# Layer 3 of a four-layer graph network: powers of the transition matrix replaced by Horner's rule

## The chip, the cores and the metric

The kernel runs on one core of a Trainium2 chip. The metric is the device time of one execution in microseconds (us). Of the kernel before there are three timed runs (median 2751.52 us, 2751.24 to 2751.78) and one profiled execution, whose trace is what everything here is read from. Differences below about 0.2% of this time can't be told from no change.

The engines are named as in the profile: PE is TensorE's matmul, PEld its weight load, DVE is VectorE, ACT is ScalarE, POOL is GpSimd, SP is the queue that issues nearly all transfers. Each engine works off its own instruction queue in order, and engines wait for each other by semaphores.

## The reference

A batch of 128 graphs of 64 nodes with 512 features passes through four layers. Each layer normalizes its input, applies a relu, and adds the result of a graph layer to `x`. Layers 0 to 2 are attention-like layers and are not touched. Layer 3 is a diffusion with two steps:

```python
e = jax.nn.leaky_relu(sj[:, None, :] + si[:, :, None] + ab[0], negative_slope=0.2)
alpha_matrix = A * jnp.exp(e)
transition = alpha_matrix / (jnp.sum(alpha_matrix, axis=-1, keepdims=True) + 1e-12)
Xk = X
for k in range(Wk.shape[0]):
    H = H + Xk @ Wk[k] + bk[k]
    Xk = jnp.einsum('bij,bjd->bid', transition, Xk)
return jax.nn.relu(H)
```

With P for the transition, H = X W0 + P X W1 + P P X W2 + biases. `sj` and `si` are two projections of X to one number for each node.

## The kernel before

All arithmetic is in float32. The 8192 tokens are worked in 32 blocks of 256 tokens: four graphs, two tiles of 128 partitions with two graphs of 64 nodes each. Layers 0 and 1 are done in pairs of blocks, then layer 2 for all blocks, then layer 3 for all blocks. The output of each layer goes to DRAM and is loaded again. Layer 3 of block 0 begins while layer 2 of its last two blocks (30 and 31) is still under way, since `layer3_in(0)` and `layer3_step(0)` are called from the loop over layer 2.

A product of a block's 256 x 512 activations with a 512 x 512 weight is done by Strassen's scheme in Winograd's form: seven quarter-size products, numbered 1 to 7, from four sums of the activations (`sums`, L215 to L218, on POOL) and four sums of the weight (formed once). The class `Product` issues them: two matmuls for each quarter product, accumulated in two PSUM banks, `ab` and `dc`. `keep_ab` and `keep_dc` (L275, L276, L283) copy half-done results aside, and `store` (L297 to L301) adds the pieces into the result. `side_by_side` runs two products at once and calls other work between their parts. There are four banks with the tag `mm`, so two products are open at a time. Further PSUM tiles have the tags `tr` and `sc`, two banks each.

Layer 3 of a block is spread over several functions. `layer3_norm` loads `x` and the adjacency, normalizes (L168 to L180), and takes the two projections (four instructions on L787, each a product of two SBUF tiles summed along the row). `layer3_in` spreads the projection over each graph with a matmul (L392, `sm_j`), makes the transition matrix, puts it into a block-diagonal 128 x 128 tile `bd`, gets its transpose and the transpose of its square by matmuls with `bd` (L833, `pn`), and multiplies both with the normalized activations (L849, `pz`, 16 matmuls of 64 rows), which gives PX and PPX, feature-major, in `z`. It then makes the four sums of Strassen's scheme for X, PX and PPX, twelve POOL instructions. `layer3_out` accumulates the three products X W0, PX W1 and PPX W2 in the same two banks, so that only one result is taken out (L276, L283, L878 to L890), then the relu and the sum with x (L895), then the store to `out` (L901). `layer3_step(b)` interleaves `layer3_out(b)` with `layer3_in(b + 1)` and `layer3_norm(b + 2)`. A scheduler places the instructions of each engine in its queue; where it moved something that matters, the text says so.

The tile `x` has four buffers. The load of block b + 4 (L58) can be issued only when the store of block b (L901) has landed.

Helpers that the change uses: `neighbour_sums` (L384) multiplies a tile of two graphs with the transposed adjacency weights in four matmuls of 64 x 64 x 512, each in another quadrant of TensorE; layers 0 and 1 use it (tiles `pa` and `po`). Layer 1 also takes its row sums with matmuls against a column of ones (L575, `den`), and `load_adjT` loads the transposed adjacency.

Of the kernel before, what the change touches and what calls it, by code (L numbers as in the profile page):

```python
# [8 lines left out]
FP = mybir.dt.float32  # L9
AF = mybir.ActivationFunctionType  # L10
# [15 lines left out]
def kernel(ctx: ExitStack, tc: tile.TileContext, a: dict, out: bass.AP):  # L26
# [22 lines left out]
    def tokens(ap):  # L49
        return ap.rearrange("(t p) d -> p t d", p=P)  # L50


    def rows(b: int):
        return slice(b * T, (b + 1) * T)
# [6 lines left out]
    def load_adjT(b: int, stage: int):  # L61
        adjT = med.tile([P, TT, N], FP, tag="adjT", name=f"adjT{stage}_{b}")
        nc.sync.dma_start(adjT, tokens(adjT_d[rows(b), :]))
        return adjT
# [36 lines left out]
    def weight(name: str, place: int, queue):  # L101
        w = fetched(name, place, queue)
        formed(w, nc.gpsimd)
        return w
# [40 lines left out]
        nc.vector.tensor_copy(eye[h, :], ident[h, h])  # L145
    neghalf = const.tile([P, TT], FP, tag="neghalf", name="neghalf")
    nc.gpsimd.memset(neghalf, -0.5)


    n_bd = 2  # L150
    bds = []
    for i in range(n_bd):
        e = const.tile([P, TT, P], FP, tag=f"bd{i}", name=f"bd{i}")
        nc.gpsimd.memset(e, 0.0)
        bds.append(e)
    turn = [0]

    def next_bd():
        turn[0] += 1
        return bds[turn[0] % n_bd]  # L160


    def norm(x, name: str):
# [225 lines left out]
    def graph_sums(e, cols: int, name: str):  # L389

        ps = ps_sc.tile([P, cols], FP, tag="sc", name=f"sm_{name}")
        nc.tensor.matmul(ps, ones_bd, e, start=True, stop=True)  # L392
        return ps
# [381 lines left out]
    def layer3_norm(b: int, source):  # L775


        x = load_x(b, source, 3)
        adj = med.tile([P, TT, N], FP, tag="adjT", name=f"adj3_{b}")
        nc.sync.dma_start(adj, tokens(adj_d[rows(b), :]))  # L780
        us, c3, _ = made3
        hs = norm(x, f"3_{b}")
        sij = small.tile([P, 2, TT], FP, tag="sij", name=f"sij_{b}")
        for s in range(2):
            for t in range(TT):
                hu = med.tile([P, D], FP, tag="agg", name=f"hu_{b}_{s}_{t}", bufs=2)
                nc.vector.scalar_tensor_tensor(  # L787
                    hu, hs[t], 1.0, us[s], ALU.mult, ALU.mult,
                    accum_out=sij[:, s, t : t + 1],
                )  # L790
        dj = small.tile([P, TT, N], FP, tag="e", name=f"dj_{b}")
        nc.vector.tensor_tensor(
            dj,
            eye.unsqueeze(1).to_broadcast([P, TT, N]),
            sij[:, 0, :].unsqueeze(2).to_broadcast([P, TT, N]),
            ALU.mult,
        )
        si = small.tile([P, TT], FP, tag="sj", name=f"si_{b}")
        nc.vector.tensor_scalar(si, sij[:, 1, :], c3, None, ALU.add)
        return x, adj, hs, dj, si  # L800

    def layer3_in(b: int, x, adj, hs, e, si, made: list):

        pj = graph_sums(e.rearrange("p t j -> p (t j)"), TT * N, f"j_{b}")
        hT = transposed(hs, f"3_{b}")
        nc.vector.tensor_tensor(
            e,
            pj.rearrange("p (t j) -> p t j", t=TT),  # L810
            si.unsqueeze(2).to_broadcast([P, TT, N]),
            ALU.add,
        )
        nc.vector.scalar_tensor_tensor(e, e, 0.2, e, ALU.mult, ALU.max)
        nc.scalar.activation(e, e, AF.Exp)
        nc.vector.tensor_tensor(e, e, adj, ALU.mult)
        den = small.tile([P, TT], FP, tag="den", name=f"den_{b}")
        nc.vector.tensor_reduce(den, e, AX.X, ALU.add)
        nc.vector.tensor_scalar(den, den, 1e-12, None, ALU.add)
        nc.vector.reciprocal(den, den)  # L820
        bd = next_bd()
        for g in range(2):
            h = slice(g * N, (g + 1) * N)
            nc.vector.tensor_tensor(
                bd[h, :, h], e[h], den[h].unsqueeze(2).to_broadcast([N, TT, N]), ALU.mult
            )
        yield
        tt = med.tile([P, TT, 2, N], FP, tag="tt", name=f"tt_{b}", bufs=2)
        for power in range(2):

            pn = ps_sc.tile([P, TT, N], FP, tag="sc", name=f"pn{power}_{b}")
            for t in range(TT):
                nc.tensor.matmul(  # L833
                    pn[:, t, :], bd[:, t, :], tt[:, t, 0, :] if power else eye,
                    start=True, stop=True,
                )
            nc.scalar.copy(tt[:, :, power, :], pn)
            yield
        z = big.tile([P, 2, K, T], FP, tag="qk", name=f"z_{b}")
        pz = [  # L840
            ps.tile([P, 2, K, N], FP, tag=tag, name=f"pz_{b}_{t}_{g}")
            for t, (ps, tag) in enumerate(((ps_tr, "tr"), (ps_sc, "sc")))
            for g in range(2)
        ]
        for t in range(TT):
            for c in range(K):
                for g in range(2):
                    h = slice(g * N, (g + 1) * N)
                    nc.tensor.matmul(  # L849
                        pz[t * 2 + g][:, :, c, :], hs[t][h, c * P : (c + 1) * P], tt[h, t],  # L850
                        start=True, stop=True,
                    )
        for i in range(2 * TT):
            nc.scalar.copy(z[:, :, :, i * N : (i + 1) * N], pz[i])

        other = ("e2", "pT", "pT" if b % 2 else "e2")
        made.append((x, [
            sums(m, f"3_{b}_{i}", ("S", other[i]))
            for i, m in enumerate((hT, z[:, 0], z[:, 1]))
        ]))  # L860
        yield

    def layer3_out(b: int, x, ops, stages):

        p = Product(f"y3_{b}")
        for i in range(3):
            p.early(ops[i], w3[i], (1, 6), i == 2)
        p.keep_ab()
        next(stages, None)
        for which in (5, 4):  # L870
            for i in range(3):
                p.early(ops[i], w3[i], (which,), i == 2)
            next(stages, None)
        p.keep_dc()

        bs = made3[2]
        y = big.tile([P, TT, D], FP, tag="v", name=f"y_{b}")
        nc.vector.tensor_tensor(y[:, 1, :F], p.d, bs[:, :F], ALU.add)  # L878
        nc.gpsimd.tensor_tensor(y[:, 0, F:], p.u2, bs[:, F:], ALU.add)
        nc.gpsimd.tensor_tensor(y[:, 1, F:], p.p5, bs[:, F:], ALU.add)  # L880
        for which in (2, 7, 3):
            for i in range(3):
                p.early(ops[i], w3[i], (which,), i == 2)
        nc.vector.tensor_tensor(p.u3, p.b, p.p1, ALU.add)
        y1 = y[:, 1, :].rearrange("p (j f) -> p j f", j=2)
        nc.vector.tensor_tensor(
            y1, y1, p.u3.unsqueeze(1).to_broadcast([P, 2, F]), ALU.add
        )
        nc.vector.tensor_tensor(y[:, 0, :F], p.a, bs[:, :F], ALU.add)
        nc.vector.tensor_tensor(y[:, 0, F:], p.c, y[:, 0, F:], ALU.add)  # L890

        to, last = tokens(out[rows(b), :]), b + 1 == n_blk
        whole = slice(0, D)
        for t, f in (1, whole), *([(0, slice(0, F)), (0, slice(F, D))] if last else [(0, whole)]):
            nc.vector.scalar_tensor_tensor(  # L895
                x[:, t, f], y[:, t, f], 0.0, x[:, t, f], ALU.max, ALU.add
            )
            if last:
                nc.sync.dma_start(to[:, t, f], x[:, t, f])
        if not last:  # L900
            nc.sync.dma_start(to, x)  # L901

# [61 lines left out]
            made2 = next(setup)  # L964


    w3, made_in = [], []
    made3 = normed3 = None

    def layer3_step(b: int, ahead: bool = True):  # L970


        nonlocal normed3
        stages = layer3_in(b + 1, *normed3, made_in) if b + 1 < n_blk else iter(())
        next(stages, None)
        if b + 2 < n_blk and ahead:
            normed3 = layer3_norm(b + 2, x2[b + 2])
        layer3_out(b, *made_in.pop(0), stages)

    qk, ops = layer2_in(0, normed2[0], [[], [end for _, end in open_end]])  # L980
    next(setup)
# [1 line left out]
    *_, v = values(0, ops)  # L983
    next(setup)
    turned2(1)
    w3 += [weight(f"L3_Wk{i}", 2 + i, nc.sync) for i in range(2)]
    for b in range(n_blk):
        x, adjq = loaded2[b]
        es = layer2_scores(b, adjq, qk)
# [6 lines left out]
        if b + 1 < n_blk:  # L996
            qk, ops = layer2_in(b + 1, normed2[b + 1])
        else:
            layer3_step(0, False)
        if b == n_blk - 2:  # L1000
            w3.append(weight("L3_Wk2", 4, nc.sync))
            next(stages)
        pTs = layer2_turned(b, es)
        if b + 1 < n_blk:
            prepare2(b + 2)
            coming = values(b + 1, ops)
            next(coming)
        next(stages, None)
        cT = layer2_context(b, v, pTs)
        part = out_part(b, x, cT)  # L1010
        if b + 1 < n_blk:
# [9 lines left out]


    for b in range(1, n_blk):
        layer3_step(b)


# [61 lines left out]
```

## Time and profile before

| what | value |
|---|---|
| timed runs, median (lowest to highest) | 2751.52 us (2751.24 to 2751.78) |
| profiled execution, its own time | 2750.76 us |
| profiled execution, span from first to last instruction | 2749.0 us |
| mean granted TensorE clock | 0.996 of full speed |
| weight loads, PEld, busy | 2352.7 us (86%) |
| layer 3 alone, 2060 to 2720 us: PE busy | 660.0 of 660 us |
| same stretch: DVE, ACT, POOL busy | 382.7, 167.8, 320.0 us |
| same stretch: DMA engines busy, mean | 14% |

The table's first rows differ a little: the profiled execution took 0.76 us less than the median of the timed runs, and its span leaves out 1.76 us around the instructions. A float32 matmul stands in the trace as two instructions; a group of `x24` is twelve matmuls. Durations of matmuls overlap in the trace, so the time that a group takes is read from the start of one group to the start of the next.

### The profile page before, as it was taken

How to read it: one execution, taken by the hardware profiler on the slowest of the kernel's cores; microseconds unless marked ns; L12 is line 12 of the kernel's file. 1: busy time of each engine (PE TensorE's matmuls, PEld its weight loads, DVE VectorE, ACT ScalarE, POOL GpSimd, SP SyncE). 2: the span in 40 equal slices, each digit the busy share in tenths (PEclk: the TensorE clock that was granted, in tenths of full speed). 3: DMA queues.
4: the chain of work that ended last, by engine and by line, in shares of the span. 5: the costliest groups of instructions: out<-in, count | busy, mean ns of one | idle time of the engine just before them, and what ended most of it. 6: DMA issues, size and time to landing. Idle time of an engine off the chain costs nothing.

```text
span 2749.0 us, 53245 instructions
## 1 busy us (share of the span) xinstructions
PE 2696.7 (98%) x21336; PEld 2352.7 (86%) x21336; DVE 1628.3 (59%) x4105; ACT 895.0 (33%) x2132; POOL 1279.6 (47%) x1648
## 2 busy tenths in 40 slices
PE   7899999999999999999999999999989999999999
PEld 5688888888888887899999999999878888888888
DVE  4466666666656667565655655556546555565553
ACT  2233333333333333333333333333322222222221
POOL 2433434343333436555555555554455444444443
PEclk9999999999999999999999999999999999999999
DMA  4111101001111113111111111111111111111110
GB/s 143 40 42 34 49 33 34 34 34 34 44 39 41 41 34 102 38 36 36 53 36 43 46 36 53 36 36 53 48 49 58 57 50 50 50 50 50 50 49 31
DMA packets 102488, 128.53 MB, mean 47 GB/s; under 512 B 40544, under 2 KB 50016, under 8 KB 102240
## 3 DMA queue, kind: packets, MB, share of 16 engines
q1 hardware_dynamic: 100576, 123.02, 13.3%
q8 instruction: 168, 2.75, 0.4%
q10 hardware_dynamic: 1664, 2.10, 0.2%
q14 instruction: 80, 0.66, 0.1%
HBM read 74.76 MB, written 50.33 MB: 46 GB/s over the span
## 4 chain that ended last, share of the span: by engine, by line
PE 87%; DVE 6%; POOL 3%; ACT 2%; DMA 1%; issue 1%; SPq 0%; DVEq 0%; ACTq 0%; POOLq 0%
PE ab_y L250 12%; PE ab_v L250 10%; PE dc_y L250 9%; PE dc_v L250 7%; PE ab_q L243 4%; PE ab_k L243 4%; PE tr L191 4%; PE ab_o L250 4%; PE ab_g L250 4%; PE dc_k L243 3%; PE dc_q L243 3%; PE dc_o L250 3%; PE ab_g L243 3%; PE dc_g L250 2%; PE pz L849 2%; PE dc_g L243 2%
## 5 line engine op out<-in xcount | busy, mean ns | idle before, releaser
L180 ACT ACTIVATE h<-x,nmr,rstd 128x512 f32<-128x512 f32 x256 | 196.5, 807 | 197.8 <-DVE nmr L175 197.6
L173 POOL TENSOR_TENSOR rstd<-ve,neghalf 128x2 f32<-128x2 f32 x128 | 89.4, 699 | 351.3 <-DVE ve L171 351.2
L250 PE MATMUL ab_v<-L_Wv,hT 128*128 128x256 f32 x768 | 200.6, 384 | 2.3 <-DVE u_v L276 1.3
L250 PE MATMUL ab_v<-L_Wv,S 128*128 128x256 f32 x768 | 198.5, 381 | 0.8 <-POOL S L216 0.8
L250 PE MATMUL dc_v<-L_Wv,S 128*128 128x256 f32 x768 | 197.6, 380 | 0.0
L250 PE MATMUL ab_y<-L_Wk,S 128*128 128x256 f32 x768 | 187.3, 380 | 0.0
L168 DVE BATCH_NORM_STATS2 stats<-x 128x6 f32<-128x512 f32 x256 | 165.4, 679 | 27.3 <-DMA x<-x 22.0
L250 PE MATMUL dc_y<-L_Wk,S 128*128 128x256 f32 x768 | 177.9, 381 | 0.0
L194 ACT COPY hT<-tr 128x512 f32<-128x512 f32 x128 | 74.7, 584 | 304.3 <-PE tr L191 280.2
L215 POOL TENSOR_TENSOR S<-hT 128x256 f32<-128x256 f32 x128 | 108.2, 845 | 130.5 <-ACT hT L194 125.0
L250 PEld LDWEIGHTS ab_v<-L_Wv,S 128*128 128x128 f32 x768 | 147.0, 192 | 21.8 <-POOL S L216 1.6
L250 PEld LDWEIGHTS ab_y<-L_Wk,S 128*128 128x128 f32 x768 | 146.5, 191 | 20.1
L250 PEld LDWEIGHTS dc_v<-L_Wv,S 128*128 128x128 f32 x768 | 146.4, 191 | 20.1
L250 PEld LDWEIGHTS dc_y<-L_Wk,S 128*128 128x128 f32 x768 | 143.6, 190 | 18.2
L191 PE MATMUL tr<-ident,h 128*128 128x128 f32 x1024 | 142.5, 280 | 15.5 <-ACT h L180 13.2
L196 DVE COPY hT<-tr 128x512 f32<-128x512 f32 x128 | 87.5, 684 | 110.6 <-PE ab_v L250 106.7
L250 PEld LDWEIGHTS ab_v<-L_Wv,hT 128*128 128x128 f32 x768 | 135.1, 193 | 16.5 <-DVE u_v L276 1.7
L678 POOL TENSOR_TENSOR e<-e,r 128x512 f32<-128x512 f32 x64 | 66.4, 1058 | 163.8 <-DVE r L677 163.8
L191 PEld LDWEIGHTS tr<-ident,h 128*128 128x128 f32 x1024 | 116.2, 142 | 28.9 <-ACT h L180 23.1
L250 PE MATMUL ab_y<-L_Wk,z 128*128 128x256 f32 x512 | 126.3, 379 | 0.0
L787 DVE SCALAR_TENSOR_TENSOR hu<-h,u 128x512 f32<-128x512 f32 x128 | 100.2, 817 | 27.2 <-ACT h L180 27.0
L301 POOL TENSOR_TENSOR gv<-u_g,p_g 128x256 f32<-128x256 f32 x32 | 23.3, 729 | 198.7 <-DVE u_g L298 198.7
(273 smaller groups left out, 6574.8 us busy)
## 6 DMA issues: line engine op xcount, KB each, us to landing
x<-x SPq DMA_DIRECT2D x128, 512.0 KB, 3.4
x<-in_x_dram SPq DMA_DIRECT2D x32, 512.0 KB, 3.6
out_dram<-x SPq DMA_DIRECT2D x31, 512.0 KB, 2.7
adjq<-in_adj_dram SPq DMA_DIRECT2D x64, 64.0 KB, 2.4
L_Wk<-in_L_Wk_dram SPq DMA_DIRECT2D x16, 256.0 KB, 4.2
adjT<-in_adjT_dram SPq DMA_DIRECT2D x32, 64.0 KB, 1.9
L_Wv<-in_L_Wv_dram SPq DMA_DIRECT2D x8, 256.0 KB, 5.3
adj<-in_adj_dram SPq DMA_DIRECT2D x32, 64.0 KB, 2.0
```

What stands on the lines that cost most here:

```text
L168: nc.vector.bn_stats(stats[:, t, :], x[:, t, :])
L173: nc.gpsimd.tensor_tensor(rstd, ve, neghalf, ALU.pow)
L180: nc.scalar.activation(h, x[:, t, :], AF.Relu, bias=nmr[:, t : t + 1], scale=rstd[:, t : t + 1])
L191: nc.tensor.transpose(pt[:, k, :], h[:, k * P : (k + 1) * P], ident)
L194: nc.scalar.copy(ht, pt)
L196: nc.vector.tensor_copy(ht, pt)
L215: nc.gpsimd.tensor_tensor(S1, A21, A22, ALU.add)
L243: nc.tensor.matmul(dst[:, m * P : (m + 1) * P], w[:, place, k, m * P : (m + 1) * P], left[:, k, :], start=key not in self.begun, stop=last ...
L250: nc.tensor.matmul(dst, left[:, k, :], w[:, place, k, :], start=key not in self.begun, stop=last and k == 1, skip_group_check=True,)
L678: nc.gpsimd.tensor_tensor(eh, eh, r.unsqueeze(2).to_broadcast([P, TT * hq, N]), ALU.mult)
L787: nc.vector.scalar_tensor_tensor(hu, hs[t], 1.0, us[s], ALU.mult, ALU.mult, accum_out=sij[:, s, t : t + 1],)
L849: nc.tensor.matmul(pz[t * 2 + g][:, :, c, :], hs[t][h, c * P : (c + 1) * P], tt[h, t], start=True, stop=True,)
```

## The change

Layer 3 is evaluated from the inside out: H = X W0 + P (X W1 + P (X W2)). All three products take X as their left operand, so only X is transposed and summed. The matrix product with P is done on token-major results, 128 x 512, by `neighbour_sums` in four quadrants, twice for each block (`po2` and `po3`). P isn't formed: the unnormalized weights `al`, transposed, are used, and the row sums, from four small matmuls `den`, divide afterwards (a per-partition scalar `r`). The tiles `bd`, `tt` and `z`, the matmuls `pn` and `pz`, their ACT copies, and eight of the twelve POOL sums go.

A step now has three parts. `layer3_head` runs the products X W2 and X W1 side by side, into `y12`. `layer3_tail` runs the product X W0, the row sums, and the first neighbour sum, which DVE scales by `r` and adds to X W1. `layer3_end` runs the second neighbour sum; ACT scales it, POOL adds X W0, DVE applies the relu and adds to x, and the store follows. The end of a block is called in the middle of the next block's head.

```diff
-        adj = med.tile([P, TT, N], FP, tag="adjT", name=f"adj3_{b}")
-        nc.sync.dma_start(adj, tokens(adj_d[rows(b), :]))
+        adjT = load_adjT(b, 3)
...
-        nc.vector.tensor_tensor(e, e, adj, ALU.mult)
-        den = small.tile([P, TT], FP, tag="den", name=f"den_{b}")
-        nc.vector.tensor_reduce(den, e, AX.X, ALU.add)
...
-            nc.vector.tensor_tensor(
-                bd[h, :, h], e[h], den[h].unsqueeze(2).to_broadcast([N, TT, N]), ALU.mult
-            )
+        al = small.tile([P, TT, N], FP, tag="am", name=f"al_{b}", bufs=2)
+        nc.vector.tensor_tensor(al, e, adjT, ALU.mult)
         yield
...
+        made.append((x, al, sums(transposed(hs, f"3_{b}"), f"3_{b}")))
+        yield
+
+    def layer3_head(b: int, ops, between):
+        y = big.tile([P, 2, TT, D], FP, tag="qk", name=f"y12_{b}")
+        side_by_side(*(
+            (ops, w3[i], None, lambda p, i=i: p.store(y[:, i - 1]), f"y{i}_{b}") for i in (2, 1)
+        ), between=between)
+        return y
+
+    def layer3_tail(b: int, al, ops, y):
+        p = Product(f"y0_{b}")
+        p.first(ops, w3[0])
+        p.second(ops, w3[0])
...
+        po = [ps_sc.tile([P, D], FP, tag="sc", name=f"po2_{b}_{t}") for t in range(TT)]
+        parts = neighbour_sums(po, al, [y[:, 1, t, :] for t in range(TT)])
+        r = small.tile([P, TT], FP, tag="r1", name=f"r3_{b}")
+        for t in range(TT):
+            nc.vector.tensor_scalar(r[:, t : t + 1], den[t], 1e-12, None, ALU.add)
+        nc.vector.reciprocal(r, r)
+        for t, to, at in parts:
+            nc.vector.scalar_tensor_tensor(
+                y[to, 0, t, :], po[t][at], r[at, t : t + 1], y[to, 0, t, :], ALU.mult, ALU.add
+            )
+        bs = made3[2]
+        y0 = big.tile([P, TT, D], FP, tag="v", name=f"y0_{b}")
+        nc.gpsimd.tensor_tensor(p.u2, p.u2, bs[:, F:], ALU.add)
+        nc.gpsimd.tensor_tensor(p.p5, p.p5, bs[:, F:], ALU.add)
         yield
+        p.late(ops, w3[0])
+        nc.vector.tensor_tensor(y0[:, 0, :F], p.a, bs[:, :F], ALU.add)
+        nc.vector.tensor_tensor(p.u3, p.b, p.p1, ALU.add)
+        nc.vector.tensor_tensor(y0[:, 1, :F], p.d, p.u3, ALU.add)
+        nc.gpsimd.tensor_tensor(y0[:, 1, F:], p.u3, p.p5, ALU.add)
+        nc.vector.tensor_tensor(y0[:, 0, F:], p.c, p.u2, ALU.add)
+        nc.gpsimd.tensor_tensor(y0[:, 1, :F], y0[:, 1, :F], bs[:, :F], ALU.add)
+        yield r, y0
+
+    def layer3_end(b: int, x, al, y, r, y0):
+        po = [ps_sc.tile([P, D], FP, tag="sc", name=f"po3_{b}_{t}") for t in range(TT)]
+        tz = [med.tile([P, D], FP, tag="pT", name=f"tz_{b}_{t}", bufs=3) for t in range(TT)]
         to, last = tokens(out[rows(b), :]), b + 1 == n_blk
+        for t, out_at, at in neighbour_sums(po, al, [y[:, 0, t, :] for t in range(TT)]):
+            nc.scalar.activation(tz[t][out_at], po[t][at], AF.Copy, scale=r[at, t : t + 1])
+        for t in range(TT):
+            nc.gpsimd.tensor_tensor(tz[t], tz[t], y0[:, t, :], ALU.add)
             nc.vector.scalar_tensor_tensor(
+                x[:, t, :], tz[t], 0.0, x[:, t, :], ALU.max, ALU.add
             )
...
+        y = layer3_head(b, ops, [[begin], [ending.pop()], [lambda: next(stages, None)]])
+        yield
+        tail = layer3_tail(b, al, ops, y)
+        next(tail)
+        yield
+        r_y0 = next(tail)
+        ending.append(lambda: layer3_end(b, x, al, y, *r_y0))
```

As built, the queues of steps 3 to 28 repeat. TensorE's queue for one step b is: products 1 and 6 of X W2, the spread of the projection (`sm_i`), products 5 and 4 of X W2, then 1, 6, 5, 4 of X W1, the second neighbour sum of block b - 1 (`po3`), the late part (2, 7, 3) of X W2, eight transposes for block b + 1, the late part of X W1, products 1, 6, 5, 4 of X W0, `den`, the first neighbour sum `po2`, and the late part of X W0. On DVE, the statistics for block b + 3 stand after `keep_ab` of X W0 and before the row sums' reciprocal; the four projections stand between the instructions that take out X W0 and the next step's. On SP, the load of x for block b + 4 still follows the store of block b.

## Prediction, made before the changed kernel ran

> **What bounds the kernel now.** I read the page first, then TensorE's order of time in layer 3, then the same view for layer 1, which already has the operation that the change brings in.
>
> ```profile
> PE 2696.7 (98%) x21336; PEld 2352.7 (86%) x21336; DVE 1628.3 (59%) x4105; ACT 895.0 (33%) x2132; POOL 1279.6 (47%) x1648
> ```
>
> TensorE is busy 98% of the span, and it makes 87% of the chain that ended last. One step of layer 3 on it, from the order of time (start us, us):
>
> ```profile
> 2197.25 1.03 PE L250 MATMUL ab_y<-L_Wk,S 128*128 128x256 f32 x4
> 2198.12 0.55 PE L833 MATMUL pn<-eye,bd 128*128 128x64 f32 x4
> 2198.51 2.81 PE L250 MATMUL dc_y<-L_Wk,S 128*128 128x256 f32 x12
> ...
> 2204.28 2.06 PE L849 MATMUL pz<-tt,h 64*128 64x128 f32 x32
> 2206.27 1.13 PE L250 MATMUL ab_y<-L_Wk,hT 128*128 128x256 f32 x4
> ...
> 2214.36 1.04 PE L191 MATMUL tr<-ident,h 128*128 128x128 f32 x8
> 2215.24 1.03 PE L250 MATMUL ab_y<-L_Wk,hT 128*128 128x256 f32 x4
> ```
>
> No gap: the step repeats every 22.30 us (2192.93 to 2215.24). From start to start, a quarter-product matmul takes 0.432 us (0.865 for the `x4`, two matmuls), the 42 of them 18.13; `sm_j` 0.22; transposes 0.88; `pn` 2 x 0.39; `pz` 1.99; sum 22.00. The other 0.30 are slow edges: about 0.1 before and after `pz`, which uses 64 rows of the array, and about 0.05 around each `pn`.
>
> **Steady steps on TensorE.** The 42 matmuls, `sm` and the transposes stay: 19.23 us. `pn`, `pz` and their edges go: 3.07 us. What comes is in layer 1's trace:
>
> ```profile
> 824.88 1.03 PE L250 MATMUL dc_v<-L_Wv,hT 128*128 128x256 f32 x4
> 825.83 0.29 PE L575 MATMUL den<-ones_bd,e 64*64 64x1 f32 x8
> 825.97 1.07 PE L384 MATMUL po<-v,e 64*64 64x512 f32 x8
> 826.97 1.13 PE L250 MATMUL ab_g<-fold,hT 128*128 128x256 f32 x4
> 827.94 1.03 PE L250 MATMUL ab_g<-fold,S 128*128 128x256 f32 x4
> ```
>
> `den` 0.14, `po` 1.00, and 0.09 and 0.10 of edge (0.95 and 0.97 where 0.865 is usual). So `po3` costs 1.20, `den` with `po2` 1.34, sum 2.54. A step needs 19.23 + 2.54 = 21.77 us, 0.53 less. A rule speaks against more switches: the Trainium skill, "TensorEngine Tiling (Array Packing)", Key Properties, says that changing the tiling mode drains TensorE. It gives no price there; "TensorE: Matmul & The Clock Gate", Single matmul latency, has a constant of some 166 ns for a matmul's issue and drain. An estimate with that at four edges instead of my 0.1 gives 22.0 us a step. The rows are of the same operation in the same surroundings, so I take 0.1.
>
> From the first matmul of step 1 to the last of step 31, before takes 2745.4 - 2059.12 = 686.3 us. After: 31 x (18.13 + 2.54) + 29 x 1.10 (two steps have no `sm` and transposes) = 672.7. **Gain 13.6 us.**
>
> **Can the other engines hold 21.77?** POOL loses eight sums of 0.72 and gains four 256-column adds of 0.73 and two 128x512 adds: no bound. ACT loses four 128x512 and two small copies (2.6 us) and gains as much. DVE I laid out in its queue order with the rows' durations: some 17 us in a step, no bound either, but it is in a ring. The store of block b must land before x of block b + 4 loads; its statistics stand in DVE's queue before the row sums; behind them come the four projections, then `exp` on ACT, then the scaling of `po3` on ACT, POOL's add, DVE's relu and the next store. Before, this ring has slack (DVE idles 4.9 us on `ab_y`). Its transfer leg is seen here:
>
> ```profile
> 2192.59 0.68 DVE L895 SCALAR_TENSOR_TENSOR x<-y,x 128x512 f32<-128x512 f32 x1
> ...
> 2199.46 1.29 DVE L168 BATCH_NORM_STATS2 stats<-x 128x6 f32<-128x512 f32 x2 [0.26 <-DMA x<-x]
> ```
>
> From 2193.27 to 2199.46: 6.2 us (SP's queue keeps store, then load; the adjacency behind them is needed two steps later). DVE from the statistics to the leaky relu: statistics 1.2, aggregate, `ve` and reciprocal 0.65, two small reads of `den` 0.45, three `po2` adds (as L584, 0.75, spaced 0.68) and `nmr` 2.2, wait for `rstd` 0.1, four projections at 0.70 2.8, five 256-column ops at 0.34 1.7, two small ones 0.5: 9.6. Then `exp` 0.35; three copies of 256 columns that stand before the scaling in ACT's queue 1.0; three scaled copies, priced between the plain copy (0.585) and the activation with two operands (0.807), at 0.6: 1.9; POOL's second add 1.1 (L678's 1.04; L991's 1.27 is the other end); relu 0.7; and 0.6, since POOL's second add waits for the relu of the first tile. Sum 21.5, which is 0.3 under 21.77.
>
> The last 0.6 is lock behaviour that the trace shows: a DVE op with two SBUF inputs (L886, alone 0.68) takes 1.30 beside POOL's adds. The add of bias on POOL (`d`-quarter, two adds back to back) falls on the third projection in the same way; if POOL goes first the ring is 22.1. So a step is 21.8 to 22.1; I take 21.9, costing 29 x 0.13 = **3.8 us**. Behind the waiting statistics DVE has the adds of `po2` and the taking-out of X W0; the next step's X W1 needs those banks. The tightest is `ab`, read some 3.0 us into the next step and needed at 3.7, so the wait is covered; with 0.7 more it would be TensorE's.
>
> **Layer 2 to 3.** Here before loses time:
>
> ```profile
> 2013.27 0.76 PE L191 MATMUL tr<-ident,h 128*128 128x128 f32 x5
> 2017.93 0.49 PE L392 MATMUL sm_j<-dj,ones_bd 128*128 128x128 f32 x2 [3.90 <-DVE e L661]
> ...
> 2018.80 1.91 PE L250 MATMUL ab_y<-L_Wk,hT 128*128 128x256 f32 x4
> 2020.51 1.65 PE L250 MATMUL ab_y<-L_Wk,S 128*128 128x256 f32 x4
> ...
> 2047.81 0.66 PE L691 MATMUL tr<-ident,e 128*128 128x128 f32 x4 [3.09 <-POOL e L678]
> ```
>
> `sm_j` waits for a bank that the softmax of layer 2's last block reads; that waits for POOL's updates of x, queued behind eight sums of `z`. Those sums go, so the softmax starts with the scores; and `sm_i` stands behind 1.7 us of matmuls. I take the 3.9 as gone, with the slow 1.45 us behind it. The second softmax half no longer stands behind layer 3's `ab` in DVE's queue, so the 3.09 goes too. Walking the new queues with these durations: the scores end near 2010.0, not 2013.27 (`pz` and the two `pn` out; the transposes only move); step 0 runs unbroken, 20.7 us, to 2030.7, against 29.5 us to 2042.75; layer 2's tail takes 11.8 (about 2 us idle on copies and `S_c`) against 16.4. Step 1 starts near 2042.5, not 2059.12: **gain 16.6 us.**
>
> New is a wait in step 1. x of block 3 takes the buffer of layer 2's last block, stored only at about 2045.3, so its statistics come 6.2 us later at 2051.5. DVE's queue there has statistics, two relus and four projections ahead of taking out X W2: that ends near 2059.6, while X W0 wants the banks at 2055.6. TensorE waits 4.0, the transposes and the tail behind it. Would its clock fall too? After the 3.90 wait above eight instructions took 3.2 us where 1.73 is usual, 1.45 lost. The skill's page on the clock gate (Part 1) says that one idle window of some 3.4 us halves the rate for as long, up to 1.7, or nothing where the wait straddles windows. I take 1.4: **loss 5.4 us** (0 to 8).
>
> **The ends.** Before ends 3.6 us after its last matmul (2745.4 to 2749.0). After: `po3` 1.2, ACT 2.0, POOL's second add 1.1, relu 0.7, transfer 2.7: 7.7. **Loss 4.1.** At the start `nmr` of block 0 no longer stands behind a wait for `mcol` on DVE: gain 0.3 at most; I take it.
>
> **Sum.** -13.6 + 3.8 - 16.6 + 5.4 + 4.1 - 0.3 = -17.2 us. From the profiled execution's 2750.76 that is 2733.6 (its span of 2749.0 falls to 2731.8); from the median, 0.76 higher, 2734.3. I predict 2734.
>
> **The rivals.**
> *TensorE alone paces*, the lock falls well and step 1 hardly waits: 2734 - 3.8 - 4 = 2726. For it: the ledger's 0.3 of slack. Against: back-to-back POOL ops beat the waiting DVE op in the trace. With the forecast's own middle this is one family, 2724 to 2742: 0.75.
> *The transition gives nothing* (its waits move to other releasers): 2734 + 16.6 - 5.4 = 2745. Against: the releasers named are removed. 0.08.
> *The ring paces at some 22.5*, all scaled copies at 0.8 and POOL's adds at 1.27: 29 x 0.6 more, 2751, no change. 0.11.
> *Slower: the lock.* If POOL's adds blocked three projections of each step, 3 x 0.55 on the ring's 21.5, the step is 23.1 and the time 2734 + 29 x 1.2 = 2769. It is even with before at 22.5 a step and slower beyond 22.7. Against: two of the adds wait for results that DVE makes between those projections. 0.05.
> *The work does not shrink*: the quadrants don't overlap here. Layer 1 shows eight in 1.00 us, so 0.01; 2760.
>
> A measurement tells 0.2%, 5.5 us, from no change: faster 0.85, same 0.09, slower 0.06. The range, 2720 to 2748, takes in the first two cases and half the third, with step 1's wait from none to 8.
>
> **What would show it.** Right: TensorE without gaps in steady steps, 21.8 to 22.1 us from `po3` to `po3`; `po` 1.0 us; statistics of x waiting about 2 us for DMA in each step; no wait at step 0, one of 3 to 5 us at step 1 before X W0; some 7.7 us after the last late matmul. Wrong: a regular TensorE wait on DVE, or a step at 22.3 or more.

## The result, and the profile after

| | kernel before | changed kernel |
|---|---|---|
| timed runs, median (lowest to highest), six each | 2751.38 us (2749.5 to 2751.84) | 2735.84 us (2733.86 to 2737.46) |
| ratio, 95% interval | | 0.9943 (0.993 to 0.9956) |
| profiled execution, span | 2749.0 us | 2734.2 us |
| mean granted TensorE clock | 0.996 | 0.994 |

The change gains 15.5 us, 0.57%. The prediction was 2734.0 with a range of 2720 to 2748. The two spans differ by 14.8 us, where the prediction's sum was 17.2.

The page's first row answers to the one of before: busy time, share of the span and instructions of each engine.

```profile
PE 2678.9 (98%) x20824; PEld 2275.4 (83%) x20824; DVE 1689.9 (62%) x4360; ACT 941.9 (34%) x2228; POOL 1279.7 (47%) x1582
```

TensorE has 17.8 us less to do, VectorE 61.6 and ScalarE 46.9 us more; POOL is where it was. TensorE is still busy 98% of a shorter span. A steady step in TensorE's order of time (start us, us; the start of the next row tells how long a group took):

```profile
2279.95 1.04 PE L178 MATMUL tr<-ident,h 128*128 128x128 f32 x8
...
2286.01 1.03 PE L237 MATMUL dc_y<-L_Wk,hT 128*128 128x256 f32 x4
2286.96 0.29 PE L823 MATMUL den<-ones_bd,al 64*64 64x1 f32 x8
2287.10 1.07 PE L371 MATMUL po<-y,al 64*64 64x512 f32 x8
2288.10 1.13 PE L237 MATMUL ab_y<-L_Wk,hT 128*128 128x256 f32 x4
2289.07 1.03 PE L237 MATMUL ab_y<-L_Wk,S 128*128 128x256 f32 x4
...
2301.73 1.04 PE L178 MATMUL tr<-ident,h 128*128 128x128 f32 x8
```

From transposes to transposes it is 21.78 us, with no wait. The granted clock is 1.00 from 2100 to 2720 us in both kernels, so steady steps are compared at one clock. `po` takes 1.00 us, `den` 0.14, the edges 0.09 (0.95 from 2286.01) and 0.10 (0.97 from 2288.10), as in layer 1. Of the 28 distances between successive `sm_i` from step 2 on, 26 are 21.77 or 21.78; the other two are 22.04 and 21.85.

The same step on the other engines, in order of time, shows the ring of the prediction:

```profile
2288.21 1.29 DVE L155 BATCH_NORM_STATS2 stats<-x 128x6 f32<-128x512 f32 x2 [2.04 <-DMA x<-x]
...
2295.07 1.23 DVE L773 SCALAR_TENSOR_TENSOR hu<-h,u 128x512 f32<-128x512 f32 x1
...
2297.36 0.28 DVE L798 SCALAR_TENSOR_TENSOR di<-di 128x128 f32<-128x128 f32 x1
...
2299.14 2.09 ACT L857 ACTIVATE tz<-po,r 128x512 f32<-128x512 f32 x3 [0.28 <-PE po L371]
...
2301.37 1.65 POOL L859 TENSOR_TENSOR tz<-tz,y 128x512 f32<-128x512 f32 x1 [0.20 <-ACT tz L857]
...
2303.06 0.69 DVE L860 SCALAR_TENSOR_TENSOR x<-tz,x 128x512 f32<-128x512 f32 x1 [1.16 <-POOL tz L859]
```

Read it as a loop: relu's end to the next statistics 6.24 us (2303.75 to 2288.21 + 21.78), statistics to the end of the leaky relu 9.43, on to the scaled copies 1.50, to relu's end 4.61; together 21.78. In that loop the one wait for something that is not in it is ScalarE's, 0.28 us for `po` from TensorE. So the ring itself needs 21.50, TensorE sets the pace, and the ring is right behind it.

Step 1, the one place in layer 3 where TensorE stands for over 1 us:

```profile
2058.06 0.29 PE L823 MATMUL den<-ones_bd,al 64*64 64x1 f32 x8
2063.03 2.08 PE L237 MATMUL ab_y<-L_Wk,hT 128*128 128x256 f32 x4 [4.69 <-DVE u_y L285]
2064.90 1.91 PE L237 MATMUL ab_y<-L_Wk,S 128*128 128x256 f32 x4
2066.61 1.55 PE L237 MATMUL dc_y<-L_Wk,S 128*128 128x256 f32 x4
2068.00 1.03 PE L237 MATMUL dc_y<-L_Wk,hT 128*128 128x256 f32 x4
```

A wait of 4.69 us, and behind it three groups that take 1.87, 1.71 and 1.39 us where 0.865 is usual: 2.4 us more. The clock had fallen while TensorE still waited. The profile by stretches shows it (from:to, length, busy us of PE, PEld, DVE, ACT and POOL with the number of instructions, then the granted clock, the DMA share and GB/s):

```profile
2060.84:2063.03 2.19, 0.00 (x0) 0.00 (x0) 2.19 (x10) 0.04 (x1) 0.00 (x0) 0.50 0.43 166
2063.03:2067.67 4.64, 4.64 (x11) 3.75 (x12) 2.31 (x10) 0.37 (x1) 1.41 (x2) 0.50 0.33 113
```

Before and behind these 6.83 us the clock is 1.00. Half of the 4.64 us in which matmuls ran is the time lost. The 3.9 and 3.1 us waits of before are gone, and step 1 starts at 2044.66 instead of 2059.12.

### The profile page after: what moved, and what is told of

It reads as the page before. It is cut to its first block, busy times and chain, and to the rows that moved or that the text cites. A ratio compares the mean times of both kernels' runs of the same rounds, so it can differ in the third digit from the quotient of the medians.

```text
span 2734.2 us, 52778 instructions
## 1 busy us (share of the span) xinstructions
PE 2678.9 (98%) x20824; PEld 2275.4 (83%) x20824; DVE 1689.9 (62%) x4360; ACT 941.9 (34%) x2228; POOL 1279.7 (47%) x1582
## 4 chain that ended last, share of the span: by engine, by line
PE 85%; DVE 5%; POOL 4%; DMA 2%; ACT 2%; issue 1%; SPq 0%; POOLq 0%; ACTq 0%; DVEq 0%
PE ab_y L237 12%; PE ab_v L237 10%; PE dc_y L237 9%; PE dc_v L237 7%; PE ab_q L230 4%; PE ab_g L237 4%; PE ab_k L230 4%; PE ab_o L237 4%; PE tr L178 4%; PE po L371 3%; PE dc_k L230 3%; PE ab_g L230 3%; PE dc_q L230 3%; PE dc_o L237 3%; PE dc_g L237 3%; PE dc_g L230 2%
## 5 line engine op out<-in xcount | busy, mean ns | idle before, releaser
L237 PE MATMUL ab_y<-L_Wk,hT 128*128 128x256 f32 x768 | 205.1, 390 | 5.3 <-DVE u_y L285 4.7
L237 PEld LDWEIGHTS ab_y<-L_Wk,hT 128*128 128x128 f32 x768 | 138.5, 190 | 72.3 <-issue 25.2
L237 PE MATMUL ab_y<-L_Wk,S 128*128 128x256 f32 x768 | 198.0, 380 | 0.0
L237 PE MATMUL dc_y<-L_Wk,S 128*128 128x256 f32 x768 | 197.7, 380 | 0.0
L859 POOL TENSOR_TENSOR tz<-tz,y 128x512 f32<-128x512 f32 x64 | 91.8, 1435 | 142.7 <-ACT tz L857 140.7
L237 PEld LDWEIGHTS ab_v<-L_Wv,hT 128*128 128x128 f32 x768 | 135.1, 193 | 16.6 <-DVE u_v L263 1.8
```

The source lines that it names most:

```text
L237: nc.tensor.matmul(dst, left[:, k, :], w[:, place, k, :], start=key not in self.begun, stop=last and k == 1, skip_group_check=True,)
L859: nc.gpsimd.tensor_tensor(tz[t], tz[t], y0[:, t, :], ALU.add)
```

## Experiments

Each kernel ran beside the kernel before on its own chip; so ratios are compared, and times only roughly. Layer 3 begins up to 5 us earlier or later from one kernel's execution to another's (the same instruction, the first `sm_i`, starts at 1979.59 in the longer ring below and at 1984.34 in the kernel with held statistics). A difference of a few us between two spans is therefore looked for in the stage where the edit is.

**A fifth buffer for x.** Is step 1's wait the buffer that layer 2's last block holds?

```diff
-        x = big.tile([P, TT, D], FP, tag="x", name=f"x{stage}_{b}", bufs=4)
+        x = big.tile([P, TT, D], FP, tag="x", name=f"x{stage}_{b}", bufs=5)
```

> The changed kernel with five buffers for x instead of four. Theory: the 4.7 us wait in step 1 of layer 3 is x of block 3, which needs the buffer that layer 2's last block stores; with a fifth buffer it takes that of the block before, and the wait and the 2.4 us of slow clock behind it go. Step 1 falls from 28.0 to about 21 us, the steady step stays at 21.8 (TensorE paces it), and the time falls by some 7 us from 2735.8 to about 2729. Rival: the wait comes from the length of DVE's queue (statistics, relus, projections ahead of taking out X W2), then over 3 us of it stay and the time is 2733 or more.

Measured 2730.29 us (2729.33 to 2733.07), ratio 0.9929 (0.9917 to 0.9942). TensorE in step 1:

```profile
2060.76 1.19 PE L237 MATMUL ab_y<-L_Wk,hT 128*128 128x256 f32 x4 [2.04 <-DVE u_y L285]
2061.74 1.91 PE L237 MATMUL ab_y<-L_Wk,S 128*128 128x256 f32 x4
2063.45 1.86 PE L237 MATMUL dc_y<-L_Wk,S 128*128 128x256 f32 x4
2065.14 1.03 PE L237 MATMUL dc_y<-L_Wk,hT 128*128 128x256 f32 x4
```

The wait falls from 4.69 to 2.04, but not to nothing, and the slow clock stays: two groups at 1.71 and 1.69, at a granted clock of 0.50 (2061.70 to 2065.11). The rest is on VectorE:

```profile
2054.99 1.29 DVE L155 BATCH_NORM_STATS2 stats<-x 128x6 f32<-128x512 f32 x2 [3.48 <-DMA x<-x]
```

The scheduler used the fifth buffer to put each load and its statistics one block further ahead. So it is now the statistics of block 4 that stand in VectorE's queue at this point, and x of block 4 takes the buffer that layer 2's last block holds. In steady steps nothing changes either: statistics wait 33.3 us for their loads in the last 15 such steps (32.5 in the changed kernel), 21.78 us a step. The wait has two parts, a buffer and an in-order queue, and a buffer alone moves the queue along with it.

**The statistics of block 4 held back in step 1.** Does the other part go if VectorE's queue there holds nothing that waits?

```diff
+        if behind is not None:
+            nc.vector.tensor_copy(stats[:, :, 0], behind)
...
-                normed3 = layer3_norm(b + 2, x2[b + 2])
+                normed3 = layer3_norm(b + 2, x2[b + 2], kept.get(b - 1))
...
+        if b == 1:
+            kept[b] = y[:, 0, 1, 0:TT]
```

> The changed kernel with a fifth buffer for x (2730.3 us alone) and the statistics of block 4 held behind step 1's two higher products (two columns of the product copied into the statistics' tile, which the statistics then overwrite), so that VectorE's queue in step 1 holds nothing that waits for a load; the queues of TensorE and SyncE are those of the kernel with the fifth buffer. Theory (what is left of step 1's wait is those statistics at the head of VectorE's queue, 3.48 us for their load): the 2.04 us wait falls under 0.5 us and the some 1.7 us of slow clock behind it go; step 2 may pay under 1 us for statistics that now come in a heap: 2726 to 2728 us. Rival (the wait has another cause, or the heap stops step 2 for as long): 2730 us or more.

Measured 2730.73 us (2728.96 to 2734.52), ratio 0.9926 (0.9914 to 0.9939): no different from the fifth buffer alone. Step 1 is clean: no wait and no slow clock, 30.40 us between the two `sm_i` around it, where the fifth buffer alone has 34.38 and the changed kernel 37.72. But the next four distances are 24.40, 22.49, 21.88 and 22.27 us. Around step 2 TensorE waits twice, 1.09 us each, the second time for a bank that the first neighbour sum's add reads:

```profile
2093.75 0.49 PE L381 MATMUL sm_i<-di,ones_bd 128*128 128x128 f32 x2 [1.09 <-DVE y L836]
```

The held statistics and projections of blocks 4 and 5 come in a heap, and the statistics behind them wait 4.28 us for their load. So the theory is right about the place, the rival about the sum: of the 4.0 us won in step 1, 2.6 + 0.7 + 0.1 + 0.5 are given back in the next four.

**The scores of layer 2's last block without the POOL sums (on the kernel before).** Is it the eight sums of `z` that held the softmax? For block 0 the products take quarters of `z` in place of their four sums each, so this block's result is another one.

```diff
+            if b == 0:
+                o = dict(ops[0])
+                zz = z[:, i - 1]
+                o[1], o[2] = (zz[:, 0:2, :P], B11), (zz[:, 2:4, :P], B21)
+                o[4] = (zz[:, 2:4, P:], T4)
+                ops.append(o)
```

> The kernel before with the eight POOL sums of z left out for block 0 alone (the products of block 0 with W1 and W2 then take X's sums in their place, so their values are not the reference's; the matmuls stay in number and shape). Theory: TensorE's wait of 3.9 us at the beginning of step 0, with 1.45 us of slow clock behind it, comes from POOL's backlog of these sums ahead of layer 2's updates of x; they go, and step 0 begins some 5 us earlier: 2746. The later 3.1 us wait on the second half of the softmax may stay, since DVE's queue order causes it. Rival: DVE's queue alone delays the softmax of the last block; then the 3.9 us stay and the time is within 1 us of 2751.4.

Measured 2744.63 us (2742.01 to 2748.59), ratio 0.998 (0.9973 to 0.9987): 5.4 us faster than before on the same chip. Both waits are gone (3.90 and 3.09), and POOL begins its update of x at 2011.80, right behind the sums of X. A new wait is in step 0:

```profile
2028.04 1.09 PE L833 MATMUL pn<-eye,bd 128*128 128x64 f32 x4 [2.84 <-DVE bd L824]
```

So the sums did hold the softmax, as the prediction said. Taking them out gives 5.4 us net. The new wait and the 6.63 us behind it at a granted clock of 0.50 (2028.04 to 2034.67) take back some 6.2 of what was won (an estimate from the two: 2.84 and half of 6.63). The changed kernel has no `bd` to wait for. The other 11 us of the transition's gain weren't taken apart by a run; in the trace `pz`, `pn` and this wait are what else is gone there.

**The quadrants taken back.** Each neighbour sum is two 128x128 matmuls on a block-diagonal tile, so the quadrants' overlap is gone. TensorE's other work stays; besides, ScalarE and VectorE take each sum out in two pieces instead of three, and `al` is written in two halves.

```diff
-        for t in range(TT):
-            for g in range(2):
-                nc.tensor.matmul(
-                    ps[t][half[g ^ t]], e[half[g], t, :], us[t][half[g]], start=True, stop=True
-                )
+        for t in range(TT):
+            nc.tensor.matmul(ps[t], bd[:, t, :], us[t], start=True, stop=True)
```

> The changed kernel with one thing put back: each neighbour sum is two 128x128 matmuls of 512 columns on a block-diagonal tile (its other blocks zeroed once), not four quadrants; the denominators likewise two matmuls on a column of ones. Same outputs computed, Horner's rule kept. Theory (steady step paced by TensorE, and the quadrants' overlap is real work saved): a sum costs 1.73 us (two of the earlier kernel's 0.87 us matmuls) in place of 1.0 plus 0.2 of edges, two sums a step, so a step grows from 21.78 to about 22.8 us and the kernel from 2734 to about 2766 us. Rival (the quadrants save nothing that sets the pace, because something other than TensorE paces): steps stay near 21.8 us, 2734 us; the copies of half a tile also go, so that it could even gain a little.

Measured 2775.94 us (2774.93 to 2777.29), ratio 1.0094 (1.0077 to 1.0111). This version doesn't compute what its expectation says: with two block-diagonal tiles in turn, a block's weights are overwritten before its second sum has read them. So it ran again with three:

> The neighbour sums as block-diagonal matmuls again, now with three block-diagonal tiles in turn instead of two (with two, a block's weights were overwritten by those of two blocks later before its last sum had read them, so that the two-tile kernel computed another sum, at 2775.9 us). Instructions and sizes on TensorE are the same. Theory: the two-tile time stands: a step of 23.1 us, 2774 to 2777 us. Rival (the third tile frees a wait that was in that time): nearer the 2766 us expected of it at first.

Measured 2774.88 us (2773.3 to 2776.16), ratio 1.0085 (1.0072 to 1.0099), 23.11 us a step in all but one. In TensorE's order of time:

```profile
2299.90 0.50 PE L834 MATMUL den<-ones,bd 128*128 128x1 f32 x4
2300.26 1.96 PE L378 MATMUL po<-y,bd 128*128 128x512 f32 x4
2302.06 1.03 PE L237 MATMUL ab_y<-L_Wk,hT 128*128 128x256 f32 x4
```

The first sum takes 1.80 us and the second 1.72 (2288.67 to 2290.39) against 1.00, `den` 0.36 against 0.14, without the edges. The expectation of 22.8 a step left `den` out and took each sum for 1.73. With 1.33 us more of work TensorE still has no wait, and the kernel is 24 us slower than the one before. So the gain hangs on the quadrants: in this form, on full-size matmuls, Horner's rule loses.

**The ring made longer.** How much slack has it? One more scaled copy on ScalarE, 0.68 us, into a tile that nothing reads.

```diff
+        more = snap.tile([P, D], FP, tag="more", name=f"more_{b}")
...
+            if t == 0:
+                nc.scalar.activation(more, po[0], AF.Copy, scale=r[:, 0:1])
```

> The changed kernel with one more scaled copy of po3 (128x512, into a tile that nobody reads) ahead of the three on ACT. It lengthens the ring of store, load, statistics, projections, exp, scaling, add, relu by some 0.6 to 0.7 us a step and gives TensorE nothing to do. Theory: the ring had 0.2 to 0.3 us to spare, so the step grows from 21.78 to about 22.2 us and the time by some 10 us to 2746, with the statistics' wait for x shorter or TensorE waiting at po3 or at X W0's banks. Rival: TensorE alone paces the steps with room to spare; then the time stays within 2 us of 2735.8.

Measured 2748.51 us (2746.86 to 2752.37), ratio 0.9997 (0.9989 to 1.0005). Steps now take 22.27 us in the mean, 0.49 more, for work on an engine that is busy a third of the time. TensorE meets VectorE where the prediction put the tightest bank, in the next step's X W1:

```profile
2317.73 1.13 PE L237 MATMUL ab_y<-L_Wk,hT 128*128 128x256 f32 x4 [0.37 <-DVE u_y L844]
```

By the loop read above, 0.28 of the 0.68 us should be free and 0.40 be left; 0.49 are. The other 0.1 wasn't isolated; the scheduler also put the taking-out of X W0 (L843, L844) behind `nmr`, which waits 0.81 us for POOL. In this step ScalarE's extra copy still waits for `po` (0.29 us at 2300.09), so the chain that paces here runs from that taking-out over TensorE's X W1 and `po3` to ScalarE, not over `exp` alone.

**The block's end on VectorE.** One instruction scales and adds X W0 in place of ScalarE's copy and POOL's add.

```diff
-            nc.scalar.activation(tz[t][out_at], po[t][at], AF.Copy, scale=r[at, t : t + 1])
+            nc.vector.scalar_tensor_tensor(
+                tz[t][out_at], po[t][at], r[at, t : t + 1], y0[out_at, t, :], ALU.mult, ALU.add
+            )
...
-            nc.gpsimd.tensor_tensor(tz[t], tz[t], y0[:, t, :], ALU.add)
```

> The changed kernel with the scaling of the second neighbour sum and the addition of X W0 done in one DVE instruction for each part (three of 0.75 us, as for the first neighbour sum) instead of ACT's scaled copies and POOL's two adds. Theory: the steady step stays at 21.8 (DVE has some 4 us to spare, and the ring loses ACT's 2.1 and POOL's 1.7 us for DVE's 2.1); the end after the last late matmul falls from 8.9 to about 7.6 us; step 1's wait may grow by up to 2 us: 2734 to 2738. Rival: DVE becomes the bound, a step of over 22.3 us, 2750 or more.

Measured 2739.71 us (2738.46 to 2741.06), ratio 0.9961 (0.9949 to 0.9974). The first seven distances are 21.78, then they run from 21.81 to 22.74. That is neither the 2734 to 2738 of the theory nor the 2750 of the rival. The statistics wait longer for their load (67.9 us in 27 steps, against 58.5) and `nmr` 1.3 us for POOL. The end falls from 8.9 us to 8.5 only, where 7.6 was expected. This is argued and not tested: moving the work to the engine that carries most of the ring made the ring a little longer than TensorE's step; its slack lasted seven steps, then it paced.

**The result written elsewhere.** Does the ring close through the store? The relu writes into y0 and the store takes it from there, so x is free when VectorE has read it.

```diff
-                x[:, t, :], tz[t], 0.0, x[:, t, :], ALU.max, ALU.add
+                y0[:, t, :], tz[t], 0.0, x[:, t, :], ALU.max, ALU.add
...
-            nc.sync.dma_start(to, x)
+            nc.sync.dma_start(to, y0)
```

Three kernels: on the longer ring, on the changed kernel, and on that with the fifth buffer and the statistics of block 3 held in step 1.

> The longer ring of before (one more scaled ScalarE copy ahead of the last sum's copies, an unread tile; 2748.5 us) with one change: the block's result is written into the y0 tile and stored from there, so that x is free for the next load as soon as VectorE has read it, not when the store has landed. In the changed kernel the load was issued 2.75 us after the store (2282.00, 2284.75 us). Theory (the ring is closed through x: store, its landing, load, statistics at the head of VectorE's queue, y1, second sum, copies, add): the ring is about 2.7 us shorter, far more than the 0.68 us that was added, and TensorE paces again: 2734 to 2737 us. Rival (the ring is closed inside the engines' queues, not through x): still about 2748 us.

> The changed kernel with only that edit (the result written into y0 and stored from there; x still four buffers). Theory: TensorE already paces the steady steps at 21.78 us, so a shorter ring gives nothing there; step 1 waits for a load into a buffer that layer 2's last store holds, which this doesn't touch; so 2733 to 2736 us, and VectorE's 2.04 us wait for the statistics' load all but gone. Rival (the ring costs something in each step): 2730 or less.

> That kernel with a fifth buffer for x and the statistics of block 3 held behind the end of step 1's higher products (a copy of one column of the product into the statistics' tile, which is then overwritten). With a fifth buffer alone it was 2730.3 us, and step 1 still lost 2.04 us and a slow clock because those statistics stood in VectorE's queue 3.48 us waiting for their load. Theory (the other part of step 1's wait is VectorE's in-order queue): the wait at step 1 falls under 0.5 us and the slow clock behind it goes, 2726 to 2728 us. Rival (VectorE's queue is held by something else there, or the wait only moves to step 2): 2730 to 2732 us.

Measured, in the same order: 2765.27 us (2764.12 to 2766.67), ratio 1.0055 (1.004 to 1.007); 2775.08 (2773.66 to 2777.51), ratio 1.0091 (1.0076 to 1.0106); 2773.81 (2773.45 to 2774.99), ratio 1.0087 (1.0072 to 1.0102). All three theories and their rivals miss. In the second, TensorE and VectorE show why, each in its order of time:

```profile
2305.86 1.13 PE L237 MATMUL dc_y<-L_Wk,S 128*128 128x256 f32 x4 [0.91 <-ACT p_y L270]
```

```profile
2301.29 1.29 DVE L155 BATCH_NORM_STATS2 stats<-x 128x6 f32<-128x512 f32 x2 [1.59 <-DMA x<-x]
2302.49 0.41 DVE L263 TENSOR_TENSOR u_y<-ab_y,p_y 128x256 f32<-128x256 f32 x1
```

With the load free earlier, the scheduler put the statistics ahead of the copy out of X W0's first bank (L263), where they still wait 1.59 us, and a relu on ScalarE ahead of the copy out of its second bank (L270). TensorE's next matmuls need those two copies. So each step pays some 1.5 us (23.3 in the mean, in place of 21.78), which has nothing to do with the ring. In the third the hold did its work in step 1 (no wait before X W0, where the second has 4.61 us), but waits of 1.51, 0.74 and 2.56 us follow by the end of step 2's X W0, and then the same 23.3 a step.

**The same with the queues put back.** Each block's statistics are held behind the first copy out of X W0, by two columns of it copied into the statistics' tile.

```diff
+            nc.vector.tensor_copy(stats[:, :, 0], behind[:, 0:TT])
...
         p.first(ops, w3[0])
+        kept[b] = p.u2
```

> The result written into y0 and stored from there, as in the run that came to 2775.1 us, with each block's statistics held behind the first copy out of the y0 product (two columns of it are copied into the statistics' tile), which puts VectorE's queue and ScalarE's back so that what TensorE waits for (u2 and p5 of y0) stands ahead of the statistics and the relus. Theory (the 1.4 us a step that writing elsewhere cost is the order of two queues, not the ring): steps of 21.8 us again, 2733 to 2737 us. Rival (writing elsewhere costs by itself, by y0's buffer or another chain): 2760 us or more.

> The longer ring (the extra scaled ScalarE copy of 0.68 us, 2748.5 us) with the result written elsewhere and the statistics held in the same way: the test that the run of 2765.3 us could not make, since its queues were in another order. Theory (the ring that e3 filled closes through the store's landing and the next load into x): that chain is now about 2.7 us shorter, TensorE paces, 2734 to 2738 us. Rival (the ring closes elsewhere, inside the queues): 2746 us or more.

The first, on the changed kernel: 2734.62 us (2733.71 to 2735.37), ratio 0.9939 (0.9926 to 0.9953), all 28 distances 21.77 or 21.78. So the 40 us were the order of two queues, and a store that no longer holds x gives nothing where TensorE paces. The second, on the longer ring: 2740.67 us (2740.27 to 2741.77), ratio 0.9962 (0.9947 to 0.9977), steps of 21.95 in the mean. That lies between theory (2734 to 2738) and rival (2746 or more). The load is issued 0.47 us behind the store (2283.24, 2283.71) and not 2.75 as in the changed kernel, no statistics wait for a load, and two thirds of what the longer ring cost are recovered (22.27 to 21.95, of the way to 21.78). This speaks for a ring that closes through the store's landing, but the hold alone on the longer ring wasn't run. The rest can be a wait of the hold's own making, for `u2` with POOL's bias already added in place:

```profile
2310.55 0.67 DVE L154 COPY stats<-u_y 128x2 f32<-128x2 f32 x1 [1.77 <-POOL u_y L842]
```

Whether a hold without that wait would reach 21.78 wasn't tried.

## Why the prediction was right, and which terms were off

| term of the sum | predicted, us | trace, us |
|---|---|---|
| steady work of TensorE | -13.6 | -13.6 |
| ring and lock | +3.8 | +0.8 (remainder) |
| layer 2 to 3 | -16.6 | -14.5 |
| wait of step 1 | +5.4 | +7.1 |
| the end | +4.1 | +5.3 |
| the start | -0.3 | not seen |
| sum | -17.2 | -14.8 (spans) |

The trace's terms come from the same marks as the prediction's. Step 1's start to the last late matmul went from 686.3 us to 680.6 (2044.66 to 2725.27): -5.7. In it the wait is 4.69 + 2.4 = 7.1 and the work -13.6, so 0.8 is left over and put down to the ring, of which the two odd steps make 0.34.

*Steady work*: right to 0.01 us a step, by the prices of layer 1's own rows, edges of 0.1 included; the 22.0 of the prediction's other estimate didn't come. The block-diagonal kernel shows the other way round that this saving is the quadrants'.

*Ring and lock*: the step that failed. The prediction had the ring at "21.5, which is 0.3 under 21.77", and then took 21.9 for POOL's adds blocking a projection. The blocking came in the shown step (the projection at 2295.07 takes 1.23 us for 0.69; POOL's last add 1.65 for 1.1), and the ring still took 21.50: VectorE's leg was 9.43 us with the blocking in it, against the 9.6 priced without it. The statistics and the small instructions behind them, up to the `po2` adds, were priced at 2.3 and took 1.73 (2288.21 to 2289.94): pricing short instructions by their durations overcounts them, since they start some 0.13 us after one another (2289.41, 2289.54, 2289.69, 2289.81). VectorE's "some 17 us in a step" is overcounted in the same way: its durations add up to 16.7 us a step in the trace, and it is busy for 14.5. ScalarE, said to gain as much as it loses, has 1.4 us a step more to do (5.6 before, 7.0 after), since each of the three products is now taken out by itself; with two thirds of the step idle this cost nothing. So the rival "TensorE alone paces" describes the steady steps, and the forecast's middle does not. The longer ring agrees with the 0.28 us of slack to 0.1 us, and the fear behind the term was real too: with 0.7 more, as the prediction said, the wait is TensorE's.

*Layer 2 to 3*: the named waits went and the clock's loss with them. In the trace of after, the scores of layer 2's block 30 already start 1.7 us late (1981.02, 1979.30 before). The kernel before without the POOL sums, which has the queues of before up to there, has them at 1981.84, so this isn't the change, and the transition itself gave 16.2. Step 0, predicted unbroken at 20.7 us, took 21.3 (2012.18 to 2033.52), because of a wait that the prediction had not:

```profile
2030.83 1.13 PE L237 MATMUL ab_y<-L_Wk,hT 128*128 128x256 f32 x4 [0.60 <-DVE u_y L263]
```

Layer 2's tail took 11.1 for 11.8.

*Wait of step 1*: the place, the cause and the sign were right, the size was not. The wait was 4.69 for 4.0. The slow clock behind it took 2.4 for 1.4: the prediction reckoned with one stretch of 3.4 us at half rate, worth up to 1.7, and it was 6.83 us. The fifth buffer and the hold show both halves of the cause, load and queue.

*The end*: 8.9 us instead of 7.7 (2725.27 to 2734.2). The larger part of what was missing is POOL's second add:

```profile
2727.28 1.27 POOL L859 TENSOR_TENSOR tz<-tz,y 128x512 f32<-128x512 f32 x1
2728.72 1.66 POOL L859 TENSOR_TENSOR tz<-tz,y 128x512 f32<-128x512 f32 x1 [0.18 <-ACT tz L857]
```

1.66 us beside VectorE's relu of the first tile (2728.58), where 1.1 was taken. The transfer behind the last relu took 3.1 us (2731.11 to 2734.2) for 2.7.

That the total was right within 2 us is in part luck: the ring's error (-3.0) cancels more than half of those of the transition (+2.1), the wait (+1.7) and the end (+1.2). The fastest version run is the changed kernel with a fifth buffer, 2730.29 us; its ratio's interval (0.9917 to 0.9942) overlaps the changed kernel's (0.993 to 0.9956).

## What to carry to other kernels

Where TensorE paces, cost a rewrite by its matmuls from rows of the same shape, and then add up the ring through stores, loads and in-order queues: here the ring had 0.28 us of slack in a step of 21.78, and 0.68 us more on an idle engine took the whole gain. An edit that frees a buffer or shortens a wait can also move instructions in the queues: compare the queues' order before believing a test of the wait (it cost 40 us here, and putting the order back recovered it all). A wait has gone only when the steps behind it are no longer than before.

## What was not expected of the hardware

A wait of only 2.04 us was enough for TensorE's slow clock: in the kernel with the fifth buffer the first group behind it ran at full speed, and the next two took 1.71 and 1.69 us, 3.4 us at a granted clock of 0.50, which cost 1.7. In the changed kernel with the result written elsewhere (2775.08 us) a wait of 1.91 us (to 2116.59) was followed by 3.41 us at 0.50 (from 2117.17), and one of 1.61 (to 2091.65) by none. The 4.69 us wait cost 2.4, and two waits of 1.09 in the held kernel cost nothing beyond themselves and 0.1 of edge. The prediction cited the Trainium skill ("TensorE: Matmul & The Clock Gate", Part 1) for one idle window of some 3.4 us: the 3.4 us of half rate agree with it, the idle time needed doesn't, since 2.04 and 1.91 us did it.

A gap too short for the trace's waits still costs: in the longer ring with its queues kept, `ab` starts 0.06 us late in each step and the group behind it takes 0.97 for 0.865, 0.16 in all.
